# Layer 0's chunk sums of exponentials: accumulating DMAs from POOL in the place of VectorE additions

## The chip, the cores and the metric

The kernel runs on one core of a Trainium2 chip. The metric is the device time of one launch in microseconds, the median of the runs shown. A profile is one separate execution under the hardware profiler; its span is the time from its first to its last instruction.

## The reference

32 graphs of 512 nodes with 256 features each go through four layers that share one adjacency matrix; after each layer comes a residual and a layer norm. Layer 0 is attention with 8 heads of 32 features, layer 1 has one additive score (GAT), layer 2 has a full score matrix, layer 3 has 4 additive heads. What the change touches is layer 0:

```python
qkv = jnp.einsum('fnc,ck->fnk', x, w_qkv)
q, k, v = jnp.split(qkv, 3, axis=-1)               # 8 heads of 32
scores = jnp.einsum('fnhd,fmhd->fhnm', q, k) / jnp.sqrt(D)
scores = jnp.where(mask, scores, -1000000000.0)
attn = jax.nn.softmax(scores, axis=-1)
t = jnp.einsum('fhnm,fmhd->fnhd', attn, v).reshape(F, N, C)
x = _layernorm(x + t, ln1_g, ln1_b)
...
x = _layernorm(x + _L0_gnn_ref(x, adj, ...), axis=-1)
x = _layernorm(x + _L1_gnn_ref(x, W, a, adj), axis=-1)
x = _layernorm(x + _L2_gnn_ref(x, adj, W1, W2, W3), axis=-1)
x = _layernorm(x + _L3_gnn_ref(x, W, a, adj), axis=-1)
```

The softmax needs, for every head and target node, the sum of the masked exponentials over 512 source nodes.

## The kernel before

**Order of the work.** All 32 graphs are unrolled. Nothing is issued as the layers are written: `op(...)` records an operation with a cost for each engine that may run it, the tiles that it reads and writes, and a function that emits its instructions. `Plan.run` (line 85) then places the operations one after another on five modelled engines (PE, DVE, ACT, POOL, SP), four graphs open at a time, and emits them in that order; each engine's instructions stand in that order and wait for their inputs by semaphores. An operation's result counts as ready `LAT` after its end (line 31: 0.3 us for PE, 0.15 for DVE, 0.25 for POOL), and the slots of tiles that it was the last to use come free at the same moment (lines 165 and 169). Tiles come from fixed slots: 38 of 128 x 1040 floats ("B"), 40 small ones ("S"), 4 pairs of PSUM banks ("PS") and 6 DRAM tiles ("D").

**Layer 0** (line 511). For each of two head groups (g, four heads) and each of four chunks of 128 source nodes (c): PE makes the scores of four heads, transposed, source nodes in the partitions (`qk`, L538); ACT takes the exponential of two heads at a time out of PSUM (`ex`, L544); DVE multiplies it by the transposed 0/1 mask (`msk`, at the helper `tt`, L409). So `p[j][c]` is a tile of 128 source nodes by 2 heads x 512 target nodes, 512 KB. After chunks 1 and 3, `av` multiplies two chunks by the values on PE (L529), and then DVE adds chunk c into chunk c-1 for both head pairs j (L561 to L563, profiled at L409 as `b<-b,b`; the same row holds 96 residual additions). At the end of the group, `sums` lets PE multiply the two added-up chunks 0 and 2 by a matrix of ones (L529, `b,ones`), which gives the sums in the layout of the values. They go to SBUF and back through PE transposes (L576), their reciprocals (L582) scale the output (L590).

**Other rows that are named below.** A layer norm takes statistics on DVE (L478, L479), adds eps (L486), raises to the power -0.5 on POOL (`pow`, L488), forms the shift on DVE (L493), and normalises on ACT (L504) or DVE (L506); the result goes through PE transposes (L428) and an eviction (L406 on ACT, L404 on DVE) to the next projection (L441, L454, L643). POOL also keeps guard sums (L466 to L469) and two tensor products per graph (at L409, with `be_sb` and `g_sb`). Layers 1 and 3 write scores to a DRAM tile and load them back as a broadcast of 256 or 512 KB (L681, L687, on SP's queue); DVE makes the weights from them (L698, L801), PE uses them (L708, L809, L815). Layer 2 has L744, L748, L752, L758, L767, L775 to L786; L610 and L608 are relus of layer 0, L718 the finish of layer 1, L616 the second residual of layer 0.

Of the kernel before, what the change touches and what calls it, by code (L numbers as in the profile page):

```python
# [13 lines left out]
ALU = mybir.AluOpType  # L14
# [16 lines left out]
LAT = {"PE": 0.3, "DVE": 0.15, "ACT": 0.2, "POOL": 0.25, "SP": 4.0}  # L31


class Buf:
    __slots__ = ("tag", "t", "left", "slot", "owner", "writers", "readers")
# [4 lines left out]


class Op:
    __slots__ = ("cost", "fn", "bufs", "graph", "succ", "npred", "ready", "rank", "stage", "frees")


class Plan:
# [8 lines left out]
        self.ops, self.stage = [], 0  # L55
        self.graphs.append(self.ops)

    def op(self, cost, fn, r=(), w=(), pre=()):

        o = Op()
        o.cost, o.fn, o.graph = cost, fn, len(self.graphs) - 1
        o.succ, o.stage, o.ready = [], self.stage, 0.0
        preds = set()
        for b in r:
            preds.update(b.writers)
        for b in w:
            preds.update(b.readers)
        for b in r:  # L70
            b.readers.append(o)
        for b in w:
            b.writers.append(o)
        o.bufs = list(dict.fromkeys([*r, *w]))
        for b in o.bufs:
            b.left += 1
        o.frees = "PE" not in cost and any(b.tag == "PS" for b in r)
        o.bufs += [b for b in pre if b not in o.bufs]
        preds.discard(o)
        o.npred = len(preds)  # L80
        for p in preds:
            p.succ.append(o)
        self.ops.append(o)

    def run(self, emit=True):
        for ops in self.graphs:
            for o in reversed(ops):
                o.rank = min(o.cost.values()) + max([s.rank + 0.2 for s in o.succ], default=0.0)
        free = {e: 0.0 for e in ("PE", "DVE", "ACT", "POOL", "SP")}
        busy = dict.fromkeys(free, 0.0)  # L90
        slot_free = {t: [[0.0, s] for s in range(len(v))] for t, v in self.slots.items()}
        remaining = [len(ops) for ops in self.graphs]
        oldest, opened = 0, 0
        avail = []
        held = [{} for _ in self.graphs]

        left = []
        for ops in self.graphs:
            left.append([0] * 5)
            for o in ops:  # L100
                left[-1][o.stage] += 1

        def stage():
            return next(i for i, n in enumerate(left[oldest]) if n)

        def open_graphs():
            nonlocal opened
            while opened < len(self.graphs) and opened < oldest + self.window:
                avail.extend(o for o in self.graphs[opened] if o.npred == 0)
                opened += 1  # L110

        open_graphs()
        now = 0.0
        done_at = []
        while avail:
            cands = []
            for o in avail:
                need = {}
                for b in o.bufs:
                    if b.slot is None:  # L120
                        need[b.tag] = need.get(b.tag, 0) + 1
                s0, ok = 0.0, True
                for t, k in need.items():
                    fs = slot_free[t]
                    spare = len(fs) - k
                    if o.graph != oldest:
                        spare -= max(0, self.reserve[t][stage()] - held[oldest].get(t, 0))
                    if spare < 0:
                        ok = False
                        break  # L130
                    s0 = max(s0, sorted(f for f, _ in fs)[k - 1])
                if not ok:
                    continue
                best = None
                for e, c in o.cost.items():
                    s = max(free[e], s0, o.ready, now)
                    f = s + c
                    key = f + self.bias.get(e, 0.0)
                    if best is None or key < best[0]:
                        best = (key, s, e)  # L140
                cands.append((best[1], o, best[2]))
            assert cands, "no operation can be placed"
            tmin = min(c[0] for c in cands)
            s, o, e = min((c for c in cands if c[0] <= tmin + 0.05),
                          key=lambda c: (not c[1].frees, c[1].graph, -c[1].rank))
            now = max(now, tmin)
            f = s + o.cost[e]
            free[e] = f
            busy[e] += o.cost[e]
            for b in o.bufs:  # L150
                if b.slot is None:
                    fs = slot_free[b.tag]
                    i = min(range(len(fs)), key=lambda i: fs[i][0])
                    b.slot = fs.pop(i)[1]
                    b.t = self.slots[b.tag][b.slot]
                    b.owner = o.graph
                    held[o.graph][b.tag] = held[o.graph].get(b.tag, 0) + 1
            if emit:
                o.fn(e)
            avail.remove(o)  # L160
            for b in o.bufs:
                if o in b.readers or o in b.writers:
                    b.left -= 1
                    if b.left == 0:
                        slot_free[b.tag].append([f + LAT[e], b.slot])
                        held[b.owner][b.tag] -= 1
            for n in o.succ:
                n.npred -= 1
                n.ready = max(n.ready, f + LAT[e])
                if n.npred == 0:  # L170
                    avail.append(n)
            remaining[o.graph] -= 1
            left[o.graph][o.stage] -= 1
            if remaining[o.graph] == 0:
                done_at.append(f)
            while oldest < len(self.graphs) and remaining[oldest] == 0:
                oldest += 1
                open_graphs()
        return max(free.values()), busy, done_at
# [3 lines left out]
def kernel(  # L183
# [32 lines left out]
    nc = tc.nc  # L216
    B, N, C = x.shape
# [61 lines left out]
    with tc.tile_pool(name="pro", bufs=1) as pro, \  # L279
# [25 lines left out]
        for src, name in ((l2_w1, "l2w1"), (l2_w2, "l2w2")):  # L305
            w = load_w(pro, src, name)
# [18 lines left out]
        for w, a_sb, heads in ((l1w_sb, a1_sb, 1), (l3w_sb, a3_sb, H3)):  # L325
            d = C // heads
            for k in range(KC):
                for h in range(heads):
                    scr = pro.tile([P, C], FP, name="scr", bufs=2)
                    for o, n, scale in ((d, 0, 1.0), (d, 1, -0.8), (0, 2, 0.8)):  # L330
                        j = C + n * heads + h
# [63 lines left out]
    def T2(b):  # L395

        return b.t[:, :2 * N].rearrange("p (k n) -> p k n", k=2)
# [10 lines left out]
    def tt(e, dst, a, b, op):  # L408
        (nc.vector if e == "DVE" else nc.gpsimd).tensor_tensor(dst, a, b, op)  # L409

    op = plan.op
    EV = {"DVE": cdve(1024), "ACT": cact(1024)}
    TT = {"DVE": 1.24}
# [97 lines left out]
    def layer0(xs, xZ):  # L511
# [10 lines left out]
        for g in range(2):  # L522
# [8 lines left out]
            for c in range(NC):  # L531
                s = [Buf("PS"), Buf("PS")]

                def qk(e, g=g, c=c, s=s):
                    for j in range(2):
                        for i in range(2):
                            r = (2 * j + i) * D0
                            nc.tensor.matmul(s[j].t[:, i, :],  # L538
                                             T2(kT)[r:r + D0, g, c * P:(c + 1) * P],
                                             T2(qT)[r:r + D0, g, :], start=True, stop=True)  # L540
                op({"PE": F + 0.21}, qk, r=[qT, kT], w=s, pre=[p[0][c], p[1][c]])
                for j in range(2):
                    def ex(e, c=c, j=j, s=s, p=p):
                        nc.scalar.activation(T2(p[j][c]), s[j].t, AF.Exp, scale=SC0)  # L544
                    op({"ACT": cact(1024)}, ex, r=[s[j]], w=[p[j][c]])

                    def msk(e, c=c, j=j, p=p):
                        t = T2(p[j][c])
                        tt(e, t, t, maskT[:, c:c + 1, :].to_broadcast([P, 2, N]), ALU.mult)
                    op(TT, msk, r=[p[j][c]], w=[p[j][c]])  # L550
                if c % 2 == 1:
                    def av(e, g=g, c=c, p=p, packed=packed):
                        for m in (c - 1, c):
                            packed(p, m, lambda h: v.t[:, m * C + (4 * g + h) * D0:
                                                       m * C + (4 * g + h + 1) * D0],
                                   0, m == 0, m == NC - 1)
                    op({"PE": 2 * F + 0.13}, av, r=[v, *p[0][c - 1:c + 1], *p[1][c - 1:c + 1]],
                       w=[ps_o], pre=[oT])
                    for j in range(2):

                        op(TT, lambda e, a=p[j][c - 1], b=p[j][c]: tt(  # L561
                            e, T2(a), T2(a), T2(b), ALU.add), r=[p[j][c - 1], p[j][c]],
                            w=[p[j][c - 1]])  # L563

            def sums(e, p=p, packed=packed):
                for m in (0, 2):
# [759 lines left out]
```

## Time and profile before

| | |
|---|---|
| median of 3 runs | 3375.76 us (3374.68 to 3376.79) |
| time of the profiled execution | 3376.79 us |
| its span, first to last instruction | 3375.0 us |
| mean granted TensorE clock | 0.98 |
| chain that ended last, by engine | PE 73%, DVE 21%, ACT 2%, issue 2%, DMA 1%, SP's queue 1% |
| DMA queues | SP's 92.63 MB, 10.3% of 16 engines; no DMA is issued from POOL |

How to read it: a row of a group names line, engine, operation, output <- inputs with their shapes and the count, then busy time and mean duration in ns, then the idle time of that engine just before these instructions and what ended it. PEld is PE's loading of weights, which overlaps its matmuls. A float32 matmul of the program appears as two records. The slices are tenths of busy time in 40 equal parts of the span.

### The profile page before, as it was taken

To read this page: it belongs to the slowest core of one execution; us is meant where nothing else is said; L and a number is where in the kernel's file an instruction comes from. 1 tells how busy PE (TensorE), PEld (TensorE's weight loads), DVE (VectorE), ACT (ScalarE), POOL (GpSimd) and SP (SyncE) were. 2 spreads that over 40 slices of the span, in tenths; PEclk is the share of its full clock that TensorE was granted. 3 is DMA by queue.
4 is the path that set the end of the run, shared out by engine and by line. 5 is a ranking of instruction groups with operands and counts; after the bars stand their busy time and mean duration, and the time that the engine had idled before them with its cause. 6 is when DMAs were issued, how large, how long until landed. Compare 5 with 4: busy or idle time off the path is not lost.

```text
span 3375.0 us, 42849 instructions
## 1 busy us (share of the span) xinstructions
PE 3183.2 (94%) x16010; PEld 1740.8 (52%) x16042; DVE 2589.9 (77%) x5222; ACT 1499.7 (44%) x2139; POOL 604.7 (18%) x851
## 2 busy tenths in 40 slices
PE   5999999999999999999999999999999999999875
PEld 2355554655465455545545554554455555446443
DVE  5878779777977868787787778877877868897653
ACT  2544444435444544443554435354454444544321
POOL 0122112211210221121112122111211121121110
PEclk9999999999999999999999999999999999999987
DMA  4001111010111101110111111011001111010000
GB/s 105 1 7 35 35 32 35 16 35 20 35 38 32 32 7 35 32 35 17 35 32 25 36 32 35 16 35 32 23 26 32 29 35 35 23 31 16 29 22 20
DMA packets 191253, 100.09 MB, mean 30 GB/s; under 512 B 142528, under 2 KB 177856, under 8 KB 191040
## 3 DMA queue, kind: packets, MB, share of 16 engines
q1 hardware_dynamic: 186368, 92.63, 10.3%
q10 hardware_dynamic: 4672, 4.66, 0.5%
q8 instruction: 128, 2.10, 0.3%
q14 instruction: 85, 0.70, 0.1%
HBM read 80.15 MB, written 17.10 MB: 29 GB/s over the span
## 4 chain that ended last, share of the span: by engine, by line
PE 73%; DVE 21%; ACT 2%; issue 2%; DMA 1%; SPq 1%; POOL 0%; ACTq 0%; DVEq 0%; POOLq 0%
PE ps L441 12%; PE ps L454 10%; DVE b L409 9%; PE ps L529 7%; PE ps L775 7%; PE ps L643 6%; PE ps L744 6%; PE ps L708 5%; PE ps L809 5%; PE ps L538 5%; DVE b L801 3%; PE ps L428 3%; PE ps L815 3%; DVE s L478 2%; PE ps L767 2%
## 5 line engine op out<-in xcount | busy, mean ns | idle before, releaser
L406 ACT ACTIVATE b<-ps 128x1024 f32<-128x1024 f32 (+1 forms) x461 | 462.1, 1011 | 716.5 <-PE ps L441 184.1
L409 DVE TENSOR_TENSOR b<-b,maskT 128x1024 f32<-128x1024 f32 x512 | 618.8, 1236 | 15.4 <-ACT b L544 15.2
L544 ACT ACTIVATE b<-ps 128x1024 f32<-128x1024 f32 x512 | 490.2, 1035 | 152.7 <-PE ps L538 149.8
L488 POOL TENSOR_TENSOR s<-s,mhalf 128x4 f32<-128x4 f32 x192 | 265.9, 1388 | 1160.6 <-DVE s L486 1156.9
L409 DVE TENSOR_TENSOR b<-b,b 128x1024 f32<-128x1024 f32 x352 | 436.0, 1260 | 5.5 <-PE ps L529 4.0
L504 ACT ACTIVATE b<-b,s,s 128x256 f32<-128x256 f32 x494 | 264.4, 594 | 361.0 <-DVE s L493 335.5
L538 PE MATMUL ps<-b,b 32*128 32x512 f32 x2048 | 362.0, 649 | 27.7 <-ACT b L544 11.5
L801 DVE SCALAR_TENSOR_TENSOR b<-b,s,maskT 128x512 f32<-128x512 f32 x512 | 354.0, 761 | 16.0 <-DMA b<-r 15.8
L478 DVE BATCH_NORM_STATS2 s<-b 128x6 f32<-128x256 f32 x768 | 308.6, 402 | 1.4
L466 POOL TENSOR_TENSOR acc<-acc,s 128x4 f32<-128x4 f32 (+3 forms) x224 | 102.3, 457 | 988.1 <-DVE s L832 332.1
L809 PE MATMUL ps<-b,b 128*64 128x512 f32 x1024 | 248.4, 616 | 28.9 <-DVE b L801 28.3
L454 PE MATMUL ps<-w_sb,b 128*128 128x256 f32 x1024 | 262.9, 394 | 11.2 <-DVE b L610 8.3
L529 PE MATMUL ps<-b,b 128*32 128x512 f32 x2048 | 255.9, 602 | 2.8 <-DVE b L409 2.1
L441 PE MATMUL ps<-b,w_sb 128*128 128x512 f32 x512 | 236.2, 604 | 8.9 <-ACT b L406 8.8
L441 PE MATMUL ps<-b,wqkv_sb 128*128 128x512 f32 x512 | 235.0, 603 | 9.6 <-issue 8.3
L744 PE MATMUL ps<-b,b 128*128 128x512 f32 x512 | 240.6, 592 | 1.7
L775 PE MATMUL ps<-b,b 128*128 128x257 f32 x1024 | 233.4, 382 | 5.0 <-ACT b L406 3.4
L708 PE MATMUL ps<-b,b 128*128 128x257 f32 x1024 | 234.3, 382 | 1.0 <-DVE b L698 1.0
L538 PEld LDWEIGHTS ps<-b,b 32*128 32x128 f32 x2048 | 110.2, 185 | 223.0 <-ACT b L544 100.2
L454 PEld LDWEIGHTS ps<-w_sb,b 128*128 128x128 f32 x1024 | 185.4, 191 | 77.0 <-issue 22.0
L775 PEld LDWEIGHTS ps<-b,b 128*128 128x128 f32 x1024 | 191.8, 190 | 42.9 <-ACT b L406 7.4
L708 PEld LDWEIGHTS ps<-b,b 128*128 128x128 f32 x1024 | 191.1, 189 | 43.9 <-issue 10.8
(124 smaller groups left out, 3735.8 us busy)
## 6 DMA issues: line engine op xcount, KB each, us to landing
b<-r SPq DMA_DIRECT2D x64, 512.0 KB
b<-in_x_dram SPq DMA_DIRECT2D x256, 64.0 KB
b<-in_x_dram SPq DMA_DIRECT2D x32, 512.0 KB
out_dram<-b SPq DMA_DIRECT2D x32, 512.0 KB
b<-r SPq DMA_DIRECT2D x32, 256.0 KB
r<-s SPq DMA_DIRECT2D x128, 0.5 KB
r<-s SPq DMA_DIRECT2D x128, 2.0 KB
edge<-in_adj_dram ACTq DMA_DIRECT2D x4, 256.0 KB
```

The lines of the kernel that those rows point to most:

```text
L406: nc.scalar.activation(dst, src, AF.Copy)
L409: (nc.vector if e == "DVE" else nc.gpsimd).tensor_tensor(dst, a, b, op)
L441: nc.tensor.matmul(ps.t[:, k, :], w[:, i, col + k * P:col + (k + 1) * P], T2(xT)[:, i, :], start=(i == 0), stop=(i == KC - 1))
L454: nc.tensor.matmul(o[:, c, :], T2(xT)[:, i, c * P:(c + 1) * P], w[:, i, col:col + C], start=(i == 0), stop=(i == KC - 1 and row is None))
L529: nc.tensor.matmul(ps_o.t[D0 * h:D0 * h + D0, bank, :], lhs(h), T2(p[h // 2][c])[:, h % 2, :], start=start, stop=stop)
L538: nc.tensor.matmul(s[j].t[:, i, :], T2(kT)[r:r + D0, g, c * P:(c + 1) * P], T2(qT)[r:r + D0, g, :], start=True, stop=True)
L544: nc.scalar.activation(T2(p[j][c]), s[j].t, AF.Exp, scale=SC0)
L708: nc.tensor.matmul(ps.t[:, j, :C + 1], T2(p[m // 2])[:, m % 2, c * P:(c + 1) * P], hv.t[:, m * (C + 1):(m + 1) * (C + 1)], start=(m == 0), ...
L744: nc.tensor.matmul(ps.t[:, j, :], T2(gT)[:, i, c * P:(c + 1) * P], T2(xT)[:, i, :], start=False, stop=(i == KC - 1))
L775: nc.tensor.matmul(ps_o.t[:, j, :C + 1], t[:, m, j, :], vv()[:, m, :], start=(m == 0), stop=(m == NC - 1))
L801: nc.vector.scalar_tensor_tensor(T2(b)[:, h % 2, :], T2(R[h // 2])[:, h % 2, :], part(1)[:, 0, m, h:h + 1], maskT[:, m, :], ALU.max, ALU.m ...
L809: nc.tensor.matmul(ps_o.t[D3 * (h % 2):D3 * (h % 2 + 1), h // 2, :], T4(hv)[:, m + i, h * D3:(h + 1) * D3], T2(p[i][h // 2])[:, h % 2, :], ...
```

## The change

DVE no longer adds chunk c to chunk c-1. In its place POOL issues a DMA from the tile of chunk c to that of chunk c-1, SBUF to SBUF, 128 partitions of 4 KB, that adds to what lies there. It waits for what the addition waited for: the masks on both tiles, and the matmuls of `av` that read them. The matmuls of `sums` wait for the DMA to land. The planner is told that the operation costs POOL 1.5 us, and a new field `land` lets its result, and the slots of its tiles, count as ready 5 us later than the issue's end. All other operations and costs are as before; as the planner sees other costs, the whole order on every engine comes out anew, and with it the choice of engine for evictions, norms and relus that either ACT or DVE may run.

```diff
-    __slots__ = ("cost", "fn", "bufs", "graph", "succ", "npred", "ready", "rank", "stage", "frees")
+    __slots__ = ("cost", "fn", "bufs", "graph", "succ", "npred", "ready", "rank", "stage", "frees", "land")
...
-    def op(self, cost, fn, r=(), w=(), pre=()):
+    def op(self, cost, fn, r=(), w=(), pre=(), land=0.0):
         o = Op()
+        o.land = land
...
-                        slot_free[b.tag].append([f + LAT[e], b.slot])
+                        slot_free[b.tag].append([f + LAT[e] + o.land, b.slot])
...
-                n.ready = max(n.ready, f + LAT[e])
+                n.ready = max(n.ready, f + LAT[e] + o.land)
...
                     for j in range(2):
 
-                        op(TT, lambda e, a=p[j][c - 1], b=p[j][c]: tt(
-                            e, T2(a), T2(a), T2(b), ALU.add), r=[p[j][c - 1], p[j][c]],
-                            w=[p[j][c - 1]])
+                        op({"POOL": 1.5}, lambda e, a=p[j][c - 1], b=p[j][c]: nc.gpsimd.dma_start(
+                            a.t[:, :2 * N], b.t[:, :2 * N], accum_op=ALU.add),
+                            r=[p[j][c - 1], p[j][c]], w=[p[j][c - 1]], land=5.0)
```

One line comes in (`o.land`), so a line of the kernel before stands one line later in the changed kernel from there on: L529 becomes L530, L488 becomes L489. The accumulating DMAs stand at L562.

## The prediction

> **What bounds the kernel now.** I read the page's busy table and slices first, then the busy time by stretch, then who waited for whom on PE, then the groups around layer 0's sums.
>
> ```profile
> PE 3183.2 (94%) x16010; PEld 1740.8 (52%) x16042; DVE 2589.9 (77%) x5222; ACT 1499.7 (44%) x2139; POOL 604.7 (18%) x851
> PE   5999999999999999999999999999999999999875
> DVE  5878779777977868787787778877877868897653
> ```
>
> PE is at 9 in every slice between the prologue and the tail, while VectorE (DVE) has room in most slices. Cut at the two ends (columns: length, then busy and count for PE, PEld, DVE, ACT, POOL, then clock, DMA share, GB/s):
>
> ```profile
> 0.00:60.00 60.00, 24.10 (x64) 13.70 (x65) 28.27 (x124) 3.33 (x3) 4.77 (x55) 1.00 0.55 126
> 60.00:3200.00 3140.00, 3044.73 (x15492) 1658.97 (x15522) 2487.04 (x4917) 1457.06 (x2071) 585.70 (x770) 0.99 0.11 28
> 3200.00:3375.00 175.00, 114.40 (x458) 68.12 (x457) 74.63 (x183) 39.34 (x66) 14.22 (x26) 0.82 0.07 23
> ```
>
> From 60 to 3200 us PE is busy 3044.7 of 3140 (97%) and idle 95.3; DVE is busy 79%, POOL 19%, and the DMA engines 11%. The ends hold no layer-0 chunk sums (the last matmul of such sums starts at 3163 us), so the change can touch only this stretch. What ends PE's idle time there, longest first (who waited, for whom: us in total, times, longest):
>
> ```profile
> PE ps L809 <- DVE b L801: 14.0, 5, 5.1
> PE ps L767 <- ACT b L758: 11.7, 5, 3.9
> PE ps L538 <- ACT b L544: 11.5, 14, 2.6
> PE ps L538 <- DVE b L718: 9.8, 2, 4.9
> PE ps L454 <- DVE b L610: 8.3, 7, 1.8
> ```
>
> All releases by DVE in that list, small ones included, add up to about 51 us; ACT holds most of the rest. So removing DVE work can return 51 us of PE's visible idle time at most. Last, the groups that the change replaces, feeds and queues beside (busy, mean ns | idle time before):
>
> ```profile
> L488 POOL TENSOR_TENSOR s<-s,mhalf 128x4 f32<-128x4 f32 x192 | 265.9, 1388 | 1160.6 <-DVE s L486 1156.9
> L409 DVE TENSOR_TENSOR b<-b,b 128x1024 f32<-128x1024 f32 x352 | 436.0, 1260 | 5.5 <-PE ps L529 4.0
> ...
> L529 PE MATMUL ps<-b,ones 128*32 128x512 f32 x1024 | 129.1, 620 | 0.0
> ```
>
> The last row is the one to watch: PE never stands before the matmuls with the ones. Today the chunk sums always arrive in time.
>
> **What the Trainium skill says.** (1) "DMA: Bandwidth & Descriptors", section "SWDGE vs HWDGE vs iDMA": a DMA that accumulates can be issued from GpSimd alone, whose cores write its descriptors in software. The kernel before issues no such DMA, so its trace shows neither POOL's time for one nor its flight. (2) The same page, "Anatomy of one DMA": a price of about 2.0 us fixed plus bytes/436e3 us, most of the fixed part being the confirmation of the last write. Beside it the trace has a plain 512 KB load, the broadcast from the DRAM tile, at 3.80 us in the tail of the chain of waits; the page's price gives 2.0 + 1.2 = 3.2. (3) "SBUF — State Buffer", section "Who interferes with whom": a DVE instruction with two SBUF inputs contends with a POOL instruction that reads SBUF. The trace agrees: the DVE products at L409 have a median of 1216 ns and a maximum of 3391, beside POOL products of some 2.4 us. Descriptor writing reads no tensor, so I charge DVE nothing for it.
>
> **The change, part by part.** *Removed:* 32 graphs x 2 head groups x 2 chunk pairs x 2 head pairs = 256 additions of 1.26 us (the L409 row) = 322 us of DVE. The built order shows that the planner gives part of this back to DVE: 26 more norm steps (0.41 us each), 4 more relus, 2 more copies, 11 fewer small evictions, about +10 us net. DVE falls from 2590 to about 2280 us, 70% of the middle stretch in place of 79%. None of this is on the binding engine. Of the 51 us of PE idle time that DVE ends, I credit 30: the L801, L718 and L610 rows are delays in DVE's queue, and most of those shorten. Bounds: 0 (PE remains full, its waits pass to ACT) and 51.
>
> *Added on POOL:* 256 DMA issues. No row shows one; the nearest are the pow at 1.0 to 1.4 us (L488) and the planner's own 1.5. I take 1.0 each, 256 us, POOL going from 605 to about 860 of 3375; the bounds are 0.5 and 2.0. Capacity isn't the matter, but order is. Each DMA waits at the head of POOL's in-order queue for the matmuls that read the same tiles (L529). Behind it wait the pow of other graphs' layer norms: in the built order 47 of the 192 pow stand directly behind such a DMA. For a delayed pow wait L493 on DVE (29.4 us in 39 waits now), everything behind L493 on DVE, then L504 on ACT and the transposes on PE. 47 x 1 us of delay is 47 us; DVE and ACT stand idle 30% and 50% of the time, and other graphs' matmuls are queued on PE, so I take 10 of it, bounds 0 and 50.
>
> *Added as a wait on PE:* the sums' matmuls now wait for four DMAs, and all later matmuls wait behind them. The latency to hide, from the end of the L529 matmuls of the last chunk pair: a release of 0.3 us, two issues on POOL at 1.0, and the flight. An accumulate of 512 KB has to read 1 MB (source and old destination), by the page's price 2.0 + 2.4 = 4.4 us; two overlapping on the same 16 engines take 2.0 + 4.8 = 6.8 from the first start, of which 1.0 overlaps the second issue: so 0.3 + 2.0 + 6.8 - 1.0 = 8.1, and about 9 with the other transfers and POOL's own queue. The cover is the PE work that stands between those matmuls and the sums in the changed order. I priced it with durations of the trace of before, per record: L441 0.43 us (6.87 for 16), L454 0.23, L529 0.12, L538 0.14, L708 and L775 0.23, transposes 0.135 and so on; all of the PE program sums to 3105 at these prices, against 3183 busy. Of the 64 groups, 6 have less than 5 us of cover, 11 less than 7, 19 less than 9, 34 less than 12, 40 less than 15; the smallest is 1.1, the median 11.8. Adding up what is missing: 8 us at a latency of 5, 25 at 7, **56 at 9**, 138 at 12, 250 at 15. I take 9. The first chunk pair's DMAs have another pair of score and value matmuls as cover, and I charge them nothing; if they were late as well, the latency would be past 15.
>
> *Moved:* tiles that DVE used to release are held until a DMA lands. The planner knows of 5 us after its 1.5, so up to my 9 I charge nothing: the order has that room in it. Nothing passes SP's queue, but the 96 broadcast loads share the 16 engines. 256 x 2.4 us = 614 us of flight, 18% on top of the present 11% of DMA share; 96 x 0.18 x some 2.4 us = 41 us of later loads, for which L801 waits 15.8 us now. I take 5, bounds 0 and 30.
>
> **Sum.** The profiled execution took 3376.8 us (span 3375.0), 1.0 above the median 3375.8. From it: -30 + 10 + 56 + 5 = +41, so 3418, or 3417 from the median.
>
> **The rivals.** *The gain wins.* If an accumulate flies as fast as the plain load (3.2 to 3.8 us) and an issue costs under 1 us, the latency is about 6 and the missing cover 15 us; with the full 51 us returned the time is 3376 - 51 + 15 = 3340. For it speak DVE's 79% and PE's waits for it; against it that PE is at 97% already. It decides below a latency of about 7, where missing cover and credit are equal.
>
> *The DMA is slow in its adding.* If the engines add at half of the page's rate, a pair takes 2.0 + 9.6 = 11.6 us, the latency is about 14 and the missing cover some 210 us: 3376 - 30 + 210 + 30 = 3586. The DMA engines would then be busy over 40% of the time. For it: no row bounds the rate of adding. Against it: descriptors of 4 KB a partition over all 16 engines, the best shape for a copy.
>
> *Nothing to see.* Latency about 7: 25 + 10 - 30, within 7 us of zero.
>
> **How the numbers follow.** A measurement of this kernel can tell some 0.2%, 7 us, from no change. Chances: my forecast (3385 to 3470) 0.42; the slow adding (3470 and more) 0.22; no change 0.10; the gain 0.26. Slower 0.64, same 0.10, faster 0.26. The likeliest case's own range is 3385 to 3470. The range that should hold 8 in 10 goes from 3340, which leaves out a gain beyond the full credit, to 3590, the slow rival's middle.
>
> **What would show it.** Right: the ones matmuls at L530 (L529 now) have tens of us of idle time before them, ended by a DMA; DVE near 2280 us; PE's waits for DVE smaller; DMA share near 0.3 in the middle. If the time between issue and landing is under 5 us, or PE doesn't stand before the ones, the gain wins; if it is 10 or more, the slow rival. Wrong in its reasons: the DMAs in time but PE waiting for L504, L493 or an issue on POOL, or DVE's own work slower beside the descriptor writing.

## The result and the profile after

The changed kernel takes 3418.0 us (median of 4 runs, 3414.5 to 3424.3) against 3375.85: ratio 1.0127, 95% interval 1.011 to 1.0145. It is 42 us slower, where 41 were forecast. The profiled execution took 3419.78 us, with a span of 3417.7. How that total came about is another matter, as the experiments show.

The busy table and three rows of the slices of the changed kernel:

```profile
PE 3191.5 (93%) x16010; PEld 1749.6 (51%) x16042; DVE 2306.7 (67%) x4987; ACT 1482.1 (43%) x2118; POOL 815.3 (24%) x1107
...
PE   5899998999999999999999999999989999999975
...
DVE  5667667567686675686767769766677575687553
...
DMA  5423235132522322441333245134341242351200
```

DVE loses 283 us of busy time and gets nothing for it: PE has holes in slices 2, 7 and 30, and does its unchanged program in 3191.5 us of busy time in place of 3183.2. The same stretches as before (length, busy and count of PE, PEld, DVE, ACT, POOL, clock, DMA share, GB/s):

```profile
0.00:60.00 60.00, 23.00 (x61) 13.00 (x62) 28.21 (x123) 3.11 (x3) 4.77 (x55) 1.00 0.53 123
60.00:3200.00 3140.00, 3023.20 (x15359) 1656.43 (x15387) 2177.92 (x4625) 1427.99 (x2035) 787.54 (x1014) 0.98 0.33 70
3200.00:3418.00 218.00, 145.32 (x600) 80.21 (x594) 100.61 (x240) 50.96 (x81) 22.95 (x39) 0.82 0.10 28
```

In the middle PE's idle time goes from 95.3 to 116.8 us, and 600 matmul records are left after 3200 us where before had 458. The DMA share is 0.33, three times that of before. The new groups, kept apart by form (busy, mean ns | idle before), and the issue row of the DMA (KB, median us to landing):

```profile
L489 POOL TENSOR_TENSOR s<-s,mhalf 128x4 f32<-128x4 f32 x192 | 263.1, 1372 | 822.1 <-DVE s L487 819.7 <-DVE s L494 1.7
L562 POOL DMA_DIRECT2D b<-b x256 | 231.9, 1035 | 419.0 <-PE ps L530 381.4 <-DVE b L802 11.9 <-DVE b L405 7.8
L530 PE MATMUL ps<-b,ones 128*32 128x512 f32 x1024 | 137.3, 612 | 10.8 <-DMA b<-b 10.8
L530 PEld LDWEIGHTS ps<-b,ones 128*32 128x32 f32 x1024 | 29.1, 110 | 91.1 <-issue 66.6 <-DMA b<-b 24.1
```

```profile
b<-b POOLq DMA_DIRECT2D x256, 512.0 KB, 6.6
```

An issue costs POOL about 1.0 us, as forecast; the landing comes 6.6 us after the issue's start. But the ones matmuls, where the forecast put 56 us, show 10.8 us of idle time, in nine waits. The 24.1 us before their weight loads are not to be added to that: nine of these 17 waits are the same ones seen from PEld, and in the other eight PE was still at work on earlier matmuls. PE's list is headed by other rows:

```profile
PE ps L429 <- ACT b L505: 40.9, 19, 8.1
PE ps L442 <- DVE s L494: 17.9, 2, 11.8
PE ps L810 <- DVE b L802: 14.3, 3, 9.8
...
PE ps L530 <- DMA b<-b: 10.8, 9, 1.9
```

The first and the third of these are not new. Before has, over its whole span:

```profile
PE ps L809 <- DVE b L801: 28.3, 8, 9.5
PE ps L428 <- ACT b L504: 22.8, 12, 7.0
```

The second row is new, and it is two waits only. The longer, seen in DVE's part of the timeline:

```profile
2536.59 0.17 DVE L487 TENSOR_SCALAR s<-s 128x4 f32<-128x4 f32 x1
2549.72 1.25 DVE L515 STREAM_TRANSPOSE b<-b 128x1024 f32<-128x1024 f32 x1 [12.96 <-DMA b<-in_x_dram]
2550.89 0.12 DVE L494 SCALAR_TENSOR_TENSOR s<-s,s 128x4 f32<-128x4 f32 x1
```

and in that of SP and of PE:

```profile
2531.92 8.51 SPq L872 DMA_DIRECT2D b<-in_x_dram  x8
2540.53 2.35 SPq L864 DMA_DIRECT2D b<-in_x_dram  x1
```

```profile
2536.35 1.90 PE L530 MATMUL ps<-b,ones 128*32 128x512 f32 x16
2538.18 1.09 PE L429 MATMUL ps<-ident,b 128*128 128x128 f32 x8
2551.02 1.22 PE L442 MATMUL ps<-b,wqkv_sb 128*128 128x512 f32 x1 [11.75 <-DVE s L494]
```

The next graph's input load begins to be issued at 2531.9. Its eight issues take 8.5 us, and the transpose on DVE that needs it starts at 2549.7, 17.8 us after the first. DVE runs in order, so L494, which had nothing to do with that load, stood behind the transpose, and PE behind L494. Cut into stretches (columns as above; the DMA share adds up the times of packets, so it can pass 1), the wait shows DMA engines that are full while PE and DVE stand:

```profile
2539.30:2542.70 3.40, 0.00 (x0) 0.00 (x0) 0.00 (x0) 1.03 (x2) 0.36 (x1) 1.00 1.11 180
2542.70:2551.00 8.30, 0.00 (x0) 0.00 (x0) 1.28 (x2) 0.00 (x0) 0.00 (x0) 0.50 0.95 187
2551.00:2556.30 5.30, 5.28 (x6) 2.19 (x7) 4.99 (x12) 0.60 (x1) 0.00 (x0) 0.50 0.00 0
2556.30:2565.00 8.70, 8.70 (x30) 5.45 (x29) 1.69 (x7) 3.75 (x5) 1.04 (x1) 1.00 0.00 0
```

The list of DVE's waits for DMAs, before:

```profile
DVE b L514 <- DMA b<-in_x_dram: 68.5, 20, 8.8
DVE b L801 <- DMA b<-r: 15.8, 6, 7.5
```

and after:

```profile
DVE b L515 <- DMA b<-in_x_dram: 107.8, 23, 13.0
DVE b L802 <- DMA b<-r: 66.2, 20, 8.0
DVE b L699 <- DMA b<-r: 16.1, 3, 6.0
```

So four theories stood after the result: **W**, the forecast's main term, PE waiting for the landing; **T**, traffic that delays SP's loads; **Q**, DMAs at the head of POOL's queue that delay the pow (L494 waits 56.2 us for L489, 29.4 before); **O**, the new order itself.

### The profile page after: what moved, and what is told of

Read it like the earlier page. It is cut to its first block, busy times and chain, and to the rows that moved or that the text cites. A ratio compares the mean times of both kernels' runs of the same rounds, so it can differ in the third digit from the quotient of the medians.

```text
span 3417.7 us, 43453 instructions
## 1 busy us (share of the span) xinstructions
PE 3191.5 (93%) x16010; PEld 1749.6 (51%) x16042; DVE 2306.7 (67%) x4987; ACT 1482.1 (43%) x2118; POOL 815.3 (24%) x1107
## 3 DMA queue, kind: packets, MB, share of 16 engines
q0 software_dynamic: 36864, 134.23, 20.9%
## 5 line engine op out<-in xcount | busy, mean ns | idle before, releaser
L410 DVE TENSOR_TENSOR b<-b,maskT 128x1024 f32<-128x1024 f32 x512 | 613.2, 1231 | 51.6 <-ACT b L545 51.2
L489 POOL TENSOR_TENSOR s<-s,mhalf 128x4 f32<-128x4 f32 x192 | 263.1, 1372 | 822.1 <-DVE s L487 819.7
L505 ACT ACTIVATE b<-b,s,s 128x256 f32<-128x256 f32 x468 | 253.4, 598 | 287.4 <-DVE s L494 283.4
L539 PE MATMUL ps<-b,b 32*128 32x512 f32 x2048 | 351.0, 639 | 15.7 <-ACT b L545 7.7
L562 POOL DMA_DIRECT2D b<-b x256 | 231.9, 1035 | 419.0 <-PE ps L530 381.4
L442 PE MATMUL ps<-b,wqkv_sb 128*128 128x512 f32 x512 | 241.0, 617 | 28.5 <-DVE s L494 17.9
L530 PE MATMUL ps<-b,b 128*32 128x512 f32 x2048 | 256.0, 610 | 5.4 <-DVE b L410 3.7
L810 PE MATMUL ps<-b,b 128*64 128x512 f32 x1024 | 241.1, 608 | 14.3 <-DVE b L802 14.3
L467 POOL TENSOR_TENSOR acc<-acc,s 128x4 f32<-128x4 f32 (+3 forms) x224 | 78.3, 350 | 733.4 <-DVE s L833 241.8
L442 PE MATMUL ps<-b,w_sb 128*128 128x512 f32 x512 | 237.8, 608 | 5.1 <-ACT b L407 4.7
```

Of the source, the lines that this page charges most:

```text
L442: nc.tensor.matmul(ps.t[:, k, :], w[:, i, col + k * P:col + (k + 1) * P], T2(xT)[:, i, :], start=(i == 0), stop=(i == KC - 1))
L530: nc.tensor.matmul(ps_o.t[D0 * h:D0 * h + D0, bank, :], lhs(h), T2(p[h // 2][c])[:, h % 2, :], start=start, stop=stop)
L539: nc.tensor.matmul(s[j].t[:, i, :], T2(kT)[r:r + D0, g, c * P:(c + 1) * P], T2(qT)[r:r + D0, g, :], start=True, stop=True)
L810: nc.tensor.matmul(ps_o.t[D3 * (h % 2):D3 * (h % 2 + 1), h // 2, :], T4(hv)[:, m + i, h * D3:(h + 1) * D3], T2(p[i][h // 2])[:, h % 2, :], ...
```

## The experiments

All ratios are against the kernel before, run on the same chip, with 95% intervals. On the chip of the first four, before took 3377.7 us, so the changed kernel stands at 1.0127 x 3377.7 = 3421 there.

**e1: the changed order with no DMA at all.**

```diff
-op({"POOL": 1.5}, lambda e, a=..., b=...: nc.gpsimd.dma_start(
-    a.t[:, :2 * N], b.t[:, :2 * N], accum_op=ALU.add),
+op({"POOL": 1.5}, lambda e: None,
     r=[p[j][c - 1], p[j][c]], w=[p[j][c - 1]], land=5.0)
```

> The planned order of the changed kernel is kept, and the accumulating DMA is left out (nothing is issued in its place), so the ones matmuls sum chunks 0 and 2 alone. Whatever the DMAs cost by their wait, traffic or issue goes. W (the forecast: PE waits for the landing ahead of the ones matmuls, 56 us), T (traffic: the DMAs delay SP's loads on the shared DMA engines, DVE stands for those and PE for DVE) and Q (POOL's queue: DMAs at its head delay the pow of layer norms) all expect some 3345 us, the 30 us of credit below before. O (the new order itself is worse than the old one) expects 3400 or more.

Measured: 3349.5 us, 0.9914 (0.9897 to 0.993). The DMAs cost 3421 - 3349.5 = 71 us in this order; without them, order and relief of DVE together are worth 28. L494 still waits 54.3 us for L489 and L429 40.3 us for L505: these belong to the order, not to the DMAs. O, which expected 3400 or more, is out.

**e2: no wait for the landing.**

```diff
+ones[:, 0:1].to_broadcast([P, N]) if bank else
 T2(p[h // 2][c])[:, h % 2, :], start=start, stop=stop)
```

> Order, issues and traffic of the changed kernel, but the ones matmuls read a constant tile in the place of the added-up exponentials (so the sums are constant): PE no longer waits for a landing there. W expects 50 us less than the changed kernel, about 3365. T expects about 3405, since the loads on SP's queue are as late as before, with DVE's wait for the input load and for the broadcast near 108 and 66 us. Q expects about 3410 with the wait of L494 for L489 near 56 us.

Measured: 3400.1 us, 1.0059 (1.0042 to 1.0075). The wait is worth 3421 - 3400 = 20 us (about 12 to 29 by the two intervals), not 50, and 51 us of the DMAs' cost stay with nothing waiting for them on PE. The ones matmuls themselves keep their pace (a median of 593 ns a record here, 592 in the changed kernel). DVE's waits for the loads are as in the changed kernel:

```profile
DVE b L515 <- DMA b<-in_x_dram: 118.6, 25, 14.8
DVE b L803 <- DMA b<-r: 65.0, 20, 8.0
DVE b L700 <- DMA b<-r: 17.7, 3, 6.3
```

**e3: the same DMAs, 64 bytes a partition.**

```diff
-a.t[:, :2 * N], b.t[:, :2 * N], accum_op=ALU.add)
+a.t[:, :16], b.t[:, :16], accum_op=ALU.add)
```

> Each accumulating DMA adds 16 columns in place of 1024 (the rest of the chunk is left out of the sum): issues, waits and places in POOL's queue are as in the changed kernel, the bytes are 1/64, the flight falls to about 2 us. W expects most of its 56 us back, about 3365; T expects the same, with DVE's waits for loads back near 68 and 16 us; Q expects about 3410, with the wait of L494 for L489 near 56 us.

Measured: 3351.9 us, 0.9921 (0.9904 to 0.9937), 2 us from e1: 256 issues on POOL, their waits and their places in the queue cost nothing that can be told from zero. Q is out. Landing takes 2.3 us, and DVE's waits are those of e1:

```profile
DVE b L515 <- DMA b<-in_x_dram: 58.0, 20, 6.1
DVE b L802 <- DMA b<-r: 35.2, 13, 7.4
```

**e4: a copy in the place of the accumulate.**

```diff
-a.t[:, :2 * N], b.t[:, :2 * N], accum_op=ALU.add)
+a.t[:, :2 * N], b.t[:, :2 * N])
```

> A plain copy of the same 512 KB from POOL's queue in place of the accumulate (so only chunks 1 and 3 are summed): same issues and waits, half of the bytes read. If reading the old destination is what makes the flight 6.6 us, it falls to about 4, W and T expect a time of 3385 to 3400. If the flight is near 6 all the same, the fixed part and the company on the engines make it, and the time stays at 3410 to 3420. Q expects no change.

Measured: 3382.6 us, 1.0014 (1.0007 to 1.0021), a little better than the guess. The queue row and the issue row of this kernel:

```profile
q0 software_dynamic: 36864, 134.23, 10.2%
...
b<-b POOLq DMA_DIRECT2D x256, 512.0 KB, 3.8
```

The same row of the changed kernel has 20.9% for the same 134.23 MB: an accumulate keeps the engines busy twice as long as a copy, and lands in 6.6 us in place of 3.8. PE hardly waits at the ones matmuls here (0.8 us, before a weight load), so the 33 us above e1 are nearly all traffic. With the engine time halved, DVE's wait for the input load is 84.8 us, between 58 and 108.

**e5 and e6: an input load in larger pieces, with and without the DMAs.** If T works through the input load, that load has to matter. In both kernels it becomes one DMA in pieces of 1 KB; e6 has e1's edit besides.

```diff
-for i in range(4):
-    for k in range(KC):
-        nc.sync.dma_start(
-            T2(xZ)[32 * i:32 * i + 32, k, :].rearrange("p (j a) -> p j a", a=32),
-            v[i, :, k])
+nc.sync.dma_start(T4(xZ), x[b].rearrange("(c p) d -> p c d", p=P))
```

> The changed kernel with the transposing input load (8 DMAs per graph in pieces of 128 bytes, L872) replaced by one DMA in pieces of 1 KB, so layer 0 gets its input in another arrangement; order and everything else as in the changed kernel. To be read against e6, which has the same load and no accumulating DMA. T (traffic) by way of the input load expects DVE's wait for it (108 us in the changed kernel) to shrink to 20 or less and the cost of the DMAs, e5 less e6, to fall from 70 us to about 40. T by way of the broadcast of the scores, or W (wait at the ones matmuls), expect it to stay at 60 to 70.

> The partner of e5: the order of the changed kernel without the accumulating DMAs (chunks 0 and 2 alone are summed), with the input load in pieces of 1 KB (input in another arrangement). All theories expect e1's 3349 us less a part of DVE's 58 us of waits for the input load: 3335 to 3349.

Measured: e5 3359.7 us, 0.9948 (0.9932 to 0.9965); e6 3341.8 us, 0.9891 (0.9875 to 0.9908). The accumulating DMAs, the same 256 with 21.1% of the engines, now cost 18 us, not 71, where T had expected some 40. DVE's waits in e5:

```profile
DVE b L802 <- DMA b<-r: 64.4, 20, 7.6
DVE b L515 <- DMA b<-in_x_dram: 21.8, 12, 4.2
DVE b L699 <- DMA b<-r: 8.1, 2, 4.1
```

The waits for the broadcast are nearly as long as in the changed kernel, so they can't cost more than a part of these 18 us. The wait for the input load is down to 21.8 us, as in e6 (22.4), and with it go 53 of the 71 us. What is left, 18, has the size of W in e2, and e5's waits at the ones matmuls (11.2 us on PE) are those of the changed kernel. So in this order: some 51 us by way of the input load, 20 by the wait for the landing, and by POOL's queue nothing that can be told from zero; the intervals leave each of these up to some 8 us of room. What it is about the input load stays open in part: e5 changes the size of its pieces and the number of its issues on SP (from 8 to 1 a graph) together, and the two were not tried apart.

**e7 and e8: a planner that knows of longer loads, with the DMAs and without.** e8 has the same two edits on the kernel before.

```diff
-op({"SP": 0.8}, load, w=[xZ])
+op({"SP": 4.0}, load, w=[xZ], land=6.0)
...
-    r=[rd], w=[R[s]])
+    r=[rd], w=[R[s]], land=2.0)
```

> The changed kernel with a planner that knows of longer loads: the transposing input load costs SP's queue 4.0 us and lands 6 us later than it had assumed (0.8 and 0), the broadcast of the scores 2 us later. Nothing else changes, but the order comes out anew. T expects DVE's waits for loads to fall by half or more and some 20 us of its 48 back, about 3398. W expects 3415 to 3420.

> The kernel before (chunk sums on DVE, no accumulating DMA) with the planner told of the longer loads as in e7. If e7's gain comes from the loads alone, this takes about 3376 - 55 = 3320 as well. If it is that the DMAs' relief of DVE shows once the loads are planned for (T), this gains little, 3350 to 3376, and e7 stays ahead by the credit less the rest of the traffic.

Measured: e7 3323.0 us, 0.9834 (0.9818 to 0.9851), the fastest full version of the study; e8 3400.9 us, 1.0063 (1.0046 to 1.008), slower than before, which no theory had expected. e7 is ahead of before by more than T allows for.

**e11: e7's order with no DMA** (the edit of e1).

> The order of e7 with the accumulating DMAs left out (chunks 0 and 2 alone are summed): what the DMAs still cost when the loads are planned for. T expects that little is left, 5 to 20 us, so 3303 to 3318; if order luck made e7 fast, the DMAs still cost near 70 and this takes some 3255.

Measured: 3256.5 us, 0.9641 (0.9625 to 0.9658). The expectation of T fails: the DMAs still cost 66 us in e7's order. e7 is fast because its order, free of DMAs, is 93 us faster than the changed kernel's (3349.5 against 3256.5), and not because it bears the traffic better. Of the 93 us, 40 are less idle time of PE, and 53 are less busy time for the same matmuls: PE is busy for 3165.8 of 3345.8 us in e1 and for 3112.9 of 3253.2 in e11. The mean granted clock is 0.975 in e1 and 0.984 in e11, which by an estimate (0.9% of 3166) makes some 29 us of the 53; the rest is open. In e7 the landing shows up more at the ones matmuls (21.5 us of PE's idle time in 18 waits), and DVE's waits for the broadcast go from 12.9 us in e11 to 75.8; how the 66 us split there was not tried.

**e10: the planner told of a later landing of the sums alone.**

```diff
-op({"POOL": 1.5}, ...  land=5.0)
+op({"POOL": 1.0}, ...  land=8.0)
```

> The changed kernel with the planner told of a later landing of the accumulating DMAs alone (1.0 us of POOL and 8.0 after it, in place of 1.5 and 5.0); loads as in the changed kernel. W as a part of 20 us expects that part back and no more, about 3398; T alone expects 3410 to 3420. A time below 3380 would say that a new order by itself moves the time by tens of us.

Measured: 3436.1 us, 1.0165 (1.0148 to 1.0182): slower than the changed kernel. PE's matmuls no longer wait for these DMAs (one weight load does, for 0.8 us), yet in this order the input load is waited for even longer, and one new wait heads PE's list:

```profile
DVE b L515 <- DMA b<-in_x_dram: 186.0, 25, 20.2
```

```profile
PE ps L776 <- DVE b L663: 96.6, 6, 16.6
```

It is the input load again. In the timeline of SP, DVE and PE:

```profile
717.78 19.26 SPq L872 DMA_DIRECT2D b<-in_x_dram  x8
739.79 1.25 DVE L515 STREAM_TRANSPOSE b<-b 128x1024 f32<-128x1024 f32 x1 [19.56 <-DMA b<-in_x_dram]
741.40 2.08 PE L776 MATMUL ps<-b,b 128*128 128x257 f32 x4 [15.94 <-DVE b L663]
```

L663 stands behind the transpose on DVE, and PE behind L663; all six of the waits have this form. So e10 doesn't show what its order alone is worth.

**e9 and e9b: DMAs for the first pair of chunks only**, the second pair on DVE, with the planner as in the changed kernel (e9) and as in e7 (e9b).

```diff
+if c == 1:
     op({"POOL": 1.5}, ... nc.gpsimd.dma_start(..., accum_op=ALU.add), ..., land=5.0)
+else:
+    op(TT, ... tt(e, T2(a), T2(a), T2(b), ALU.add), ...)
```

> Only the sums of chunks 0 and 1 are made by accumulating DMAs (128 of 256), those of chunks 2 and 3 by DVE as before; the order comes out anew. The first pair has a further pair of score and value matmuls as cover. W expects no wait at the ones matmuls and half of the credit, 3362. T expects half of its 48 us less half of the credit of 28, so 3385 to 3390.

> The first pair's sums by DMA, the second's on DVE (e9), with the planner told of the longer loads (e7). T expects half of the relief and hardly any traffic cost: between e7 and e8, and about 3325. A version that beats both would be this one or e7.

Measured: e9 3343.7 us, 0.9895 (0.9878 to 0.9911); e9b 3336.7 us, 0.9873 (0.9856 to 0.9889). Both beat before. In e9 PE doesn't wait for a DMA at the ones matmuls at all, the DMA engines' extra share is 10.7%, and DVE's wait for the input load is 57.2 us, no more than e1's 58.1. e9 lies below both of its expectations; its order is new as well, and how much of the gain is the order's luck was not measured. e9b lies between e7 and e8, 12 us above T's 3325.

## Why the prediction was right in its sum and wrong in its parts

- **The credit.** "I credit 30": e1 gives 28 for relief and new order together. What the relief alone is worth isn't known; e8 against before and e11 against e1, all four without DMAs, show that a new order by itself moves this kernel by tens of us either way (+23, -93), so the agreement has luck in it.
- **POOL's issues.** 1.0 us each was right (L562). The 10 us for the pow behind them were too many: 2, not told from zero (e3). The longer waits of L494 in the trace looked like proof of it and are not; e1 has them with no DMA in the queue. That DVE was charged nothing for the issues fits: its products with the mask take 1231 ns in the mean, 1236 before. (The maximum of 3391 ns that the forecast gives for the products at L409 in before is that of the additions; the products' is 3394, and all 17 of the DVE records there over 1.8 us overlap one of POOL's products, so the reading stands.)
- **The wait on PE.** "56 at 9" is a term that was mis-sized: 20 (e2). The latency was near right: in the trace it is 8.4 us in the median from the end of a group's last `av` matmul to the landing of its last DMA (5.0 to 13.2). The count of late groups was not far off either: in 14 of the 64 groups, where 19 were forecast, the last DMA lands after the ones matmuls have begun, by 33 us in sum. But in eight of the 14 PE doesn't stand at all. The sum left out that the ones matmuls are cover themselves: half of them read chunk 0, whose DMAs landed earlier, and only the last quarter needs the last DMA. One of the six groups in which PE does stand:

```profile
2380.73 1.07 PE L530 MATMUL ps<-b,ones 128*32 128x512 f32 x8
2383.67 1.05 PE L530 MATMUL ps<-b,ones 128*32 128x512 f32 x4 [1.87 <-DMA b<-b]
2385.59 1.88 PE L530 MATMUL ps<-b,ones 128*32 128x512 f32 x4 [0.87 <-DMA b<-b]
```

So 56 us shrink to 33 by the covers and latencies of the run (the smallest cover is 3.2 us and not 1.1; why was not followed), and to 10.8 us of idle time, nine waits in six groups, by the matmuls' own cover. That e2 gives 20 and not 10.8 is in part the pace after a wait: the last four records above take 1.88 us, the same four before them 1.05.

- **The traffic.** "I take 5, bounds 0 and 30" is the step that failed outright: 51 (e2 less e1). The step had named the wrong load. It counted the 96 broadcasts, for which DVE waits some 40 us longer in e5 than in e6 (72.5 against 34.0) while the DMAs cost 18 us there in all, and said that "nothing passes SP's queue". The load that matters is the one with 4096 pieces of 128 bytes a graph: it shares the engines with pieces of 4 KB, its issues on SP back up (8.5 us for eight, 5.0 in a stretch of before), and behind it stands DVE's transpose, at a place in an in-order queue that the planner chose for a load of under 5 us. The forecast's own sign of being wrong in its reasons, PE waiting for L493 (L494 now), came true, but the input load was behind it and not an issue on POOL.
- **The rivals.** The gain would have needed the cost under the credit; it takes only the removal of that one load's pieces (e5: below before). The slow adding is half true: the accumulate does take twice the engine time of a copy (20.9% against 10.2%), which the forecast's price by bytes read had in it.

The two errors, 36 too many at the wait and 46 too few at the traffic, cancelled to within what the pow had too many. A total that is right to 1 us said nothing of its terms.

## What to carry to other kernels

Before an engine is relieved by DMAs, list what else is on the DMA engines, smallest pieces first, and ask which in-order queue has an instruction that waits for it: here most of the harm came out there, not at the reader of the new DMA. Take an addition out (e1) and shorten it (e3) before believing a wait in a trace, since waits belong to an order as much as to an operation. Where a planner lays out all queues, measure a change at a fixed order too; here new orders alone were worth from -93 to +23 us, more than the change.

## What the runs showed of the hardware beside that

- An accumulating DMA of 512 KB within SBUF: 1.0 us on POOL, 6.6 us to landing (4.5 to 12.4), and 20.9% of 16 engines for 256 of them, against 3.8 us and 10.2% for a plain copy from the same queue, and 2.3 us for 64 bytes a partition.
- A hole in PE's work can cost more than its length. In the stretches from 2539.3 us of the changed kernel, shown with the result, the granted clock is still 1.00 in the first 3.4 us of PE's idle time; it is 0.50 in the rest of it and in the first 5.3 us of work after it, and then 1.00 again. The first matmul after the wait (L442) takes 1.22 us, where the mean of its group is 0.62. The idle time comes first here, so the low clock is not its cause; that idle time brings the clock down was not tried by an experiment of its own.
- The cost shows in sums too. Between the spans of e1 and of the changed kernel (3345.8 and 3417.7 us) lie 72 us: 46 are more idle time of PE, and 26 are longer busy time for the same matmuls (3165.8 against 3191.5). The mean granted clock is 0.984 in e11, 0.980 before, 0.973 after and 0.961 in e10.
